# A four-layer graph network on one Trainium2 core: where the sums of a quantile search stand in TensorE's order, how many rows a constant has, and which engine makes the weights and second limits

## The chip, the core and the metric

The kernel runs on one core of a Trainium2 chip. The core has TensorE (PE in the profile; its weight loads are PEld), VectorE (DVE), ScalarE (ACT), GpSimd (POOL) and SyncE (SP, which here only issues DMAs). Each engine works through its own queue in order, and the engines wait for each other through semaphores. The metric is device time in microseconds (us).

## The reference, cut to what matters

Sixteen graphs of 1024 nodes and 64 channels go through four layers, each followed by a residual sum and a layer norm. Layer 0 is a normalised graph convolution, layer 1 an attention with eight heads, layer 3 a plain graph convolution. The change is in layer 2, which aggregates each node's neighbours by quantiles:

```
s = sort(where(nd, x, inf), over neighbours)     # nd: kept neighbours of a node
nv = nd.sum()                                     # their number
for tau, w in ((.25, .25), (.5, .5), (.75, .25)):
    pos = tau * max(nv - 1, 0)
    lo, hi, frac = floor(pos), ceil(pos), pos - floor(pos)
    agg += w * (s[lo] + frac * (s[hi] - s[lo]))
```

This is wanted for every node and every channel. So a pair of order statistics (`lo` and `hi`) is picked for each node, channel and one of three quantiles, and the two values are summed with the weights `w*(1-frac)` and `w*frac`.

## The kernel before, in words

The graphs are handled in pairs, eight pairs in all. One pass per pair runs layer 0, the attention, a sort of every channel over its nodes, and then the quantile search of the pair (`quantiles`, from line 880). Layers 2's small network and layer 3 of a pair are run beside layer 0 of a later pair.

**What the search does.** A channel's 1024 sorted values are cut into 32 groups of 32. A node's neighbours are a bit set over the ranks. A product of the adjacency matrix with a table `E` gives, for each node and channel, a *word*: a count of the neighbours below a group together with the bits of the group (three 16-bit words `V`). Comparing the counts with a *limit* (how many neighbours lie below the wanted order statistic) and taking differences gives a one-hot mark of the group that holds it (`lt`, then `oh`). The marked word is picked (`m = V * oh`), the 32 groups are summed (`wps`), and a bit search on VectorE (`kth_bit`) finds the place inside the group (`r2`, `r64`). From the place and the marks, products build a distance to every value of the group, ScalarE keeps what is positive (`vals`), and the sum over the group of these, together with the group's least value (`base`), is the wanted value (`acc`). The result is `acc * cf`, where `cf` is the weight.

**Steps and units.** One step treats four channels of one graph and one quantile. Eight steps form a unit; a pass has 12 units, that is 96 steps (`steps`, line 1065). The words of a step are picked 14 steps (`U8N + PARTS`) before its values are looked up. So one round `i` of the main loop (line 1116) holds, for TensorE: the sums of words of step `i-1` (`summed`, 12 products into `wps`); for the looked-up step the sums of least values (`least_values`, 4 products of `base` into `acc`), the distances (`distances`: 8 products with `pen`, 4 with `kilo`, 16 with `bd`, into four PSUM banks); one half word (`half_word`: a constant by the product `ones, magic`, then eight products `ndT, E`, into one bank); the first half of the one-hot marks of step `i+1` (`one_hot`, two products `lt, dif`, a bank each); the sums of values (`sum_values`, 4 products of `vals` with `bonesf` in float32 into `acc`); the second half of the marks; and in some rounds (three in eight) a second half word. The first step of a unit starts `acc` anew with its `least_values`, and for it these stand behind the first half of the marks, not ahead of the distances.

For VectorE a round is: the unit's result `acc * cf` if one is due (line 1055), two picks `m`, one comparison `lt` for step `i+2`, some of the next `E` tables, and, in the first six rounds of a unit, parts of `kth_bit`. ScalarE empties the PSUM banks: four `vals`, two reads of each half word into `V` (lines 947 to 953), four `oh`.

**What sets the order.** Products of the main loop go through `product`, which chains them in the order of the program, and VectorE's operations of the search go through `InOrder` (all recorded on line 749) in the same way. ScalarE's operations, and the weights and limits, are not chained: the scheduler places them. The four banks of pool `ps1` are handed out in turn, so the fifth use of a bank in a row waits for the eviction of the first. `m` has two buffers, so the first pick of a round waits for the sums of words of the round before. `acc` has one buffer.

**Limits and weights.** `rank_limits` (line 699) makes these of the neighbour counts. `limits(q)` writes `lim[:,0]` on ScalarE (line 717) and from it the two limits `s = 1, 0` on VectorE (line 719). `weights(t)` makes two 64-row `kc` and two `nvc` on ScalarE, their difference `d` on VectorE (line 731, buffer of the pool `vals`), its absolute value (line 732) and the weight `cf` (line 734), both on VectorE. For the first graph of a pair this is done ahead of the loop, but for two of the weights (rounds 10 and 12); for the second (`gr.bb` is 1) in the rounds of `SECOND`: counts in 26 and 28, weights in 30, 38 and 47, limits in 40, 45 and 46.

Of the kernel before, what the change touches and what calls it, by code (L numbers as in the profile page):

```python
# [15 lines left out]
BF = mybir.dt.bfloat16  # L16
# [4 lines left out]
AF = mybir.ActivationFunctionType  # L21
# [4 lines left out]
P = 128  # L26
# [7 lines left out]
EW = 2  # L34
# [87 lines left out]
def gnn_kernel(ctx: ExitStack, tc: tile.TileContext, a: dict, out: bass.AP):  # L122
# [52 lines left out]
    tones4 = load("tones4", [P, 4], F16, a["c_tones4"])  # L175
    kilo = const.tile([P, 1], F16, name="kilo")
    nc.vector.memset(kilo, 1024.0)
    magic = const.tile([32, EW, P], BF, name="magic")
    for w in range(EW):
        nc.vector.memset(magic[:, w], MAGIC[w] / 32)  # L180
    ones5 = const.tile([32, 512], BF, name="ones5")
    nc.vector.memset(ones5, 1.0)
    bn_a = const.tile([P, C], F32, name="bn_a")
    bn_b = const.tile([P, C], F32, name="bn_b")
# [514 lines left out]
    def rank_limits(gr, qe, qn, qm, behind):  # L699

        cnt = qe.tile([P, N], F16, name="cnt")
        gr.lim, gr.kc, gr.cf = {}, {}, {}

        def counts(hf):
            cols = slice(hf * 512, (hf + 1) * 512)
            ps = bank([P, 512])
            for j in range(NB):  # L710
                nc.tensor.matmul(ps, onesb, gr.ndT[:, j, cols], start=(j == 0), stop=(j == NB - 1))
            nc.scalar.copy(cnt[:, cols], ps)

        def limits(q):

            lim = gr.lim[q] = qe.tile([P, 2, N], U16, name="lim", bufs=LB)
            behind(nc.scalar.activation(lim[:, 0], cnt, AF.Copy, scale=0.25 * (q + 1), bias=-0.25 * (q + 1) - 0.375))
            for s in (1, 0):
                nc.vector.tensor_scalar(lim[:, s], lim[:, 0], 32.0, OFF + 32.0 * (s + 1), op0=ALU.mult, op1=ALU.add)

        def weights(t):
            nvc = qm.tile([P, 512], F16, name="nvc")
            kc = gr.kc[t] = qm.tile([P, 512], U16, name="kc", bufs=6)
            for hf in range(2):
                b = HALF[hf]
                x = cnt[b, hf * 512:(hf + 1) * 512]
                behind(nc.scalar.activation(kc[b], x, AF.Identity, scale=qrow[b, t, 0:1], bias=qrow[b, t, 1:2]))
                nc.scalar.activation(nvc[b], x, AF.Identity, bias=qrow[b, t, 4:5])

            d = qn.tile([P, 512], F32, name="vals", bufs=5)  # L730
            nc.vector.scalar_tensor_tensor(d, nvc, qrow[:, t, 0:1], kc, op0=ALU.mult, op1=ALU.subtract)
            nc.vector.scalar_tensor_tensor(d, d, -1.0, d, op0=ALU.mult, op1=ALU.max)
            cf = gr.cf[t] = qn.tile([P, 512], BF, name="cf", bufs=5)
            nc.vector.tensor_scalar(cf, d, qrow[:, t, 2:3], qrow[:, t, 3:4], op0=ALU.mult, op1=ALU.add)

        return counts, limits, weights

# [142 lines left out]
    def quantiles(ip, rk, u_w, b_w, qm, graphs):  # L880
# [12 lines left out]
        with ExitStack() as es:  # L893
# [93 lines left out]
            def summed(u, s):  # L987

                sum_words(u, s)
                if s == U8N - 1:  # L990
                    u.r2 = qn.tile([P, 512], F16, name="r2", bufs=2)
                    u.r64 = qn.tile([P, 512], F16, name="r64", bufs=2)
                    search = kth_bit(v, kb, u.wps, u.pairs[0][0].kc[u.n % 3], u.r2, u.r64)
                    next(search)
                    return search
# [51 lines left out]
            def result():  # L1047
                u = results.pop(0)
                gr = u.pairs[-1][0]
                res = qn.tile([P, 512], F32, name="vals", bufs=5)  # L1050
                if u is units[-1]:
                    nc.scalar.copy(res, u.acc)
                    nc.gpsimd.tensor_tensor(res, res, gr.cf[u.n % 3], ALU.mult)
                else:
                    searched[:] = [v.tensor_tensor(res, u.acc, gr.cf[u.n % 3], ALU.mult)]
                nc.gpsimd.dma_start(agg_d[gr.bb][:, u.n, :], res)
# [26 lines left out]
            def more_elements(n):  # L1083
                for _ in range(n):
                    if todo and made + 1 <= used // 2 + EB:
                        yield from elements()
# [25 lines left out]
            pen = qn.tile([P, U8N, 3, P], F16, name="pen")  # L1112
            nc.sync.dma_start(pen, a["c_pen"])
            lookups = [(gr, gb) for gr in graphs for gb in range(G // GB)]
            search = iter(())
            for i, (u, s) in enumerate(steps):
                if i == 3 * NQ:
                    load_matrix(graphs[1])
                if i == SECOND[0]:
                    counts, limits, weights = rank_limits(graphs[1], qe, qn, qm, behind)  # L1120
                if i in SECOND:
                    part, n = ((counts, 0), (counts, 1), (weights, 0), (weights, 1),
                               (limits, 0), (limits, 1), (limits, 2), (weights, 2))[SECOND.index(i)]
                    part(n)
                gb, at = divmod(i - U8N - 2 * NQ, GB * NQ)
                if at == 0 and gb >= 1 and lookups:
                    load_values(*lookups.pop(0))
                if i in (2, 4, 6):
                    load_values(*lookups.pop(0))
                if i in (10, 12):  # L1130
                    weights(i // 2 - 4)
                look = steps[i - U8N - PARTS] if i >= U8N + PARTS else None
                more = MORE[s] - (s == 3 and u.n % 3 == 2)
                if i:
                    search = summed(*steps[i - 1]) or search

                def large():
                    if results:
                        result()
                        yield  # L1140
                    pick(u, s, 0)
                    yield
                    pick(u, s, 1)
                    yield
                    if i + 2 < len(steps):
                        compare(*steps[i + 2])
                        yield
                    yield from more_elements(AT_ONCE[s] if i >= U8N else 2)

                runs = islice(search, RUNS[s] if s < PARTS else 0)  # L1150
                for _ in zip_longest(*((runs, large()) if s == PARTS - 1 else (large(), runs))):
                    pass
                if look and look[1]:
                    least_values(*look)
                if look:
                    distances(*look)
                more_words((more + 1) // 2)
                if i + 1 < len(steps):
                    one_hot(*steps[i + 1], 0)
                if look and not look[1]:  # L1160
                    least_values(*look)
                if look:
                    sum_values(*look)
                if i + 1 < len(steps):
                    one_hot(*steps[i + 1], 1)
                more_words(more // 2)
            search = summed(*steps[-1])
            before = None
            evicted.clear()
            for i, look in enumerate(steps[-U8N - PARTS:]):  # L1170
# [302 lines left out]
```

## Time and profile before

| | |
|---|---|
| three runs | 11837.91 us median (11832.29 to 11863.36) |
| profiled execution, its own time | 11843.83 us |
| its span, first to last instruction | 11842.1 us |
| busy in the span: PE, DVE, ACT | 10550.8, 10276.8, 7468.6 us |
| one search, first pick to last (first pair of graphs) | 1187.8 to 1972 us, about 784 us |
| mean granted TensorE clock | 0.958 |

In that first search (1187 to 1985 us) PE is busy 708.0 us of 798, DVE 756.0, ACT 526.8. A line of a waits view reads: who waited, for whom, microseconds in total, times, longest. A line of the timeline reads: start and duration in us, engine, line, operation, output<-inputs with shapes, count, and in brackets the idle time ahead of it and what ended it. A group's line has count, busy us, mean ns of one, and then the idle us ahead of its members with what ended them. Most instructions of the search have line 933 (PE) or 749 (DVE), those of the two helpers, so tiles tell them apart. The end of a matmul is modelled: starts are what can be relied on, and some matmul records are missing.

### The profile page before, as it was taken

To read this page: it belongs to the slowest core of one execution; us is meant where nothing else is said; L and a number is where in the kernel's file an instruction comes from. 1 tells how busy PE (TensorE), PEld (TensorE's weight loads), DVE (VectorE), ACT (ScalarE), POOL (GpSimd) and SP (SyncE) were. 2 spreads that over 40 slices of the span, in tenths; PEclk is the share of its full clock that TensorE was granted. 3 is DMA by queue.
4 is the path that set the end of the run, shared out by engine and by line. 5 is a ranking of instruction groups with operands and counts; after the bars stand their busy time and mean duration, and the time that the engine had idled before them with its cause. 6 is when DMAs were issued, how large, how long until landed. Compare 5 with 4: busy or idle time off the path is not lost.

```text
span 11842.1 us, 207662 instructions
## 1 busy us (share of the span) xinstructions
PE 10550.8 (89%) x81864; PEld 4573.6 (39%) x82560; DVE 10276.8 (87%) x18374; ACT 7468.6 (63%) x13812; POOL 712.4 (6%) x1212
## 2 busy tenths in 40 slices
PE   7989898998989989898898998989889998983897
PEld 4645232552335423354233542335322453221232
DVE  3588998889988899788997889988999889998996
ACT  5766666666666666566665666656666566661664
POOL 0010000000000000000000000010000100001000
PEclk8989999999999999999999999999999999996999
DMA  2021002210032000310004100041000410002001
GB/s 87 25 100 42 6 6 95 80 29 4 5 110 69 24 4 6 130 52 21 5 6 138 46 18 6 6 143 43 16 5 16 139 43 10 8 24 89 4 5 50
DMA packets 310001, 508.98 MB, mean 43 GB/s; under 512 B 120480, under 2 KB 220192, under 8 KB 306976
## 3 DMA queue, kind: packets, MB, share of 16 engines
q1 hardware_dynamic: 225296, 309.02, 8.3%
q0 software_dynamic: 50688, 99.75, 2.6%
q10 hardware_dynamic: 33040, 86.88, 2.2%
q8 instruction: 649, 10.63, 0.4%
q14 instruction: 328, 2.69, 0.1%
HBM read 379.03 MB, written 116.46 MB: 42 GB/s over the span
## 4 chain that ended last, share of the span: by engine, by line
PE 56%; DVE 27%; ACT 8%; issue 5%; DMA 3%; ACTq 0%; SPq 0%; DVEq 0%; POOL 0%
PE bank L933 19%; DVE m L749 8%; PE banks L549 7%; PE bank L571 7%; PE bank L585 7%; PE acc L933 5%; PE wps L933 3%; DVE S L749 3%; DVE lt L749 3%; ACT vals L1027 2%; DVE U L749 2%; DVE wb L749 2%; PE bank L414 1%; DVE key L1285 1%; PE bank L528 1%
## 5 line engine op out<-in xcount | busy, mean ns | idle before, releaser
L749 DVE TENSOR_TENSOR m<-V,oh 128x3072 bf16<-128x3072 bf16 x1536 | 2671.1, 1750 | 252.0 <-PE wps L933 219.1
L1027 ACT ACTIVATE vals<-bank 128x512 f32<-128x512 f32 x2848 | 1470.5, 602 | 1016.3 <-PE bank L933 1003.1
L933 PE MATMUL bank<-ndT,E 128*128 128x512 fp8e4 x7936 | 1942.2, 389 | 0.0
L556 DVE CUSTOM_DVE_ANT_0 s<-banks,adj 128x1024 f32<-128x1024 f32 x1024 | 1214.0, 1220 | 521.6 <-PE banks L549 516.4
L967 ACT CAST oh<-bank 128x512 f16<-128x512 f32 x3072 | 1591.0, 617 | 20.2 <-PE bank L933 18.6
L575 ACT COPY pT<-bank 128x512 f32<-128x512 f32 x1536 | 802.4, 593 | 812.2 <-PE bank L571 812.1
L564 ACT ACTIVATE s<-s,mx 128x1024 f32<-128x1024 f32 x1024 | 1176.4, 1160 | 98.6 <-DVE mx L556 95.9
L933 PEld LDWEIGHTS <-E 128*128 128x128 bf16 x7936 | 707.8, 99 | 1228.2 <-issue 551.2
L549 PE MATMUL banks<-kT,qT 64*128 64x512 f32 x4096 | 1113.0, 628 | 74.1 <-DVE mx L556 48.5
L571 PEld LDWEIGHTS bank<-ident,s 128*128 128x128 f32 x8192 | 900.6, 143 | 417.8 <-issue 289.7
L571 PE MATMUL bank<-ident,s 128*128 128x128 f32 x8192 | 1034.8, 280 | 8.4 <-ACT s L564 8.1
L933 PE MATMUL bank<-lt,dif 128*128 128x512 bf16 x2424 | 787.4, 383 | 262.9 <-issue 81.4
L585 PE MATMUL bank<-pT,v 128*64 128x256 f32 x8192 | 1003.8, 388 | 0.0
L749 DVE TENSOR_TENSOR lt<-V,lim 128x2048 bf16<-128x2048 uint16 x768 | 934.5, 1217 | 0.0
L933 PE MATMUL wps<-m,tonesb 128*32 128x512 bf16 x9216 | 660.8, 390 | 210.5 <-DVE m L749 208.2
L933 PE MATMUL bank<-oh,bd 64*64 64x512 f16 x11616 | 804.5, 388 | 0.0
L933 PE MATMUL acc<-vals,bonesf 128*32 128x512 f32 x5696 | 801.7, 611 | 2.2 <-ACT vals L1027 2.2
L585 PEld LDWEIGHTS bank<-pT,v 128*64 128x64 f32 x8192 | 548.1, 137 | 312.3 <-issue 47.9
L947 ACT ACTIVATE V<-bank 128x512 uint16<-128x512 f32 x512 | 305.4, 596 | 540.8 <-PE bank L933 476.8
L951 ACT ACTIVATE V<-bank 128x512 uint16<-128x512 f32 x512 | 305.5, 597 | 534.6 <-PE bank L933 533.9
L549 PEld LDWEIGHTS banks<-kT,qT 64*128 64x128 f32 x4096 | 400.1, 190 | 548.7 <-issue 341.2
L933 PE MATMUL bank<-r,pen 32*128 32x512 f16 x5808 | 587.4, 387 | 21.1 <-ACT vals L1027 13.1
(259 smaller groups left out, 14574.6 us busy)
## 6 DMA issues: line engine op xcount, KB each, us to landing
at<-in_adjT SPq DMA_DIRECT2D x256, 512.0 KB, 5.8
masks_d<-mask POOLq DMA_DIRECT2D x440, 128.0 KB, 2.0
mask<-masks_d SPq DMA_DIRECT2D x440, 128.0 KB, 2.1
adj<-in_adj SPq DMA_DIRECT2D x96, 512.0 KB, 6.0
ad<-in_adj ACTq DMA_DIRECT2D x64, 512.0 KB, 7.0
agg_d<-vals POOLq DMA_DIRECT2D x96, 256.0 KB, 2.3
agg<-agg_d ACTq DMA_DIRECT2D x16, 1536.0 KB, 7.6
nd_d<-nd SPq DMA_DIRECT2D x128, 128.0 KB, 2.1
```

The source lines that it names most:

```text
L549: then(nc.tensor.matmul(ss[h][:, hf * 512:(hf + 1) * 512], gr.qk[hp, 0][HALF[h], k * P:(k + 1) * P], gr.qk[hp, 1][HALF[h], hf * 512:(hf + ...
L556: last = nc.vector.tensor_tensor_reduce(s, ss[h], gr.adj[k], -1.0, 3.0e38, ALU.add, ALU.min, mx)
L564: then_act(nc.scalar.activation(s, s, AF.Exp, bias=mx, scale=-1.0, accum_out=sm))
L571: then(nc.tensor.transpose(ps[:, m, :], exps[h][0][:, (4 * mh + m) * P:(4 * mh + m + 1) * P], ident))
L575: then_act(nc.scalar.copy(dst, ps))
L585: then(nc.tensor.matmul(po[HALF[h]], gr.v[:, 4 * mh + m, (2 * hp + h) * C:(2 * hp + h + 1) * C], pT[h][mh][:, m, :], start=(mh == 0 and m ...
L749: i = getattr(nc.vector, name)(*args, **kw)
L933: then(nc.tensor.matmul(*args, **kw))
L947: nc.scalar.activation(gr.V[g][:, 0, cols], ps, AF.Copy, scale=2.0 ** -6, bias=OFF - MAGIC[0] / 64 - 63 / 128)
L951: nc.scalar.activation(gr.V[g][:, 2, cols], ps, AF.Copy, scale=2.0 ** -8, bias=OFF - MAGIC[1] / 256 - 255 / 512)
L967: nc.scalar.copy(u.oh[s][:, kk, cols], ps)
L1027: last = nc.scalar.activation(vals[t], ys[t], AF.Relu)
```

## The change

Four edits, the order of the first two being TensorE's own:

- The constant of a word, `magic`, gets 128 rows instead of 32 (each row a 128th of the constant instead of a 32nd), as does the vector of ones that it is multiplied with.
- The sums of values of a looked-up step stand one round later, right behind that round's sums of words; and the sums of least values (unless the step is its unit's first) right behind those, ahead of the round's vector work in the program. The unit's result on VectorE follows: it stands behind the two picks and the comparison, not ahead of them. After the loop one `sum_values` is still due and is issued behind the last sums of words.
- The two second limits of the second graph are made on ScalarE.
- The absolute value and the weight `cf` are made on ScalarE, for both graphs.

```diff
-    magic = const.tile([32, EW, P], BF, name="magic")
+    magic = const.tile([P, EW, P], BF, name="magic")
     for w in range(EW):
-        nc.vector.memset(magic[:, w], MAGIC[w] / 32)
-    ones5 = const.tile([32, 512], BF, name="ones5")
+        nc.vector.memset(magic[:, w], MAGIC[w] / P)
+    ones5 = const.tile([P, 512], BF, name="ones5")
...
             for s in (1, 0):
-                nc.vector.tensor_scalar(lim[:, s], lim[:, 0], 32.0, OFF + 32.0 * (s + 1), op0=ALU.mult, op1=ALU.add)
+                if gr.bb:
+                    nc.scalar.activation(lim[:, s], lim[:, 0], AF.Copy, scale=32.0, bias=OFF + 32.0 * (s + 1))
+                else:
+                    nc.vector.tensor_scalar(lim[:, s], lim[:, 0], 32.0, OFF + 32.0 * (s + 1),
+                                            op0=ALU.mult, op1=ALU.add)
...
             nc.vector.scalar_tensor_tensor(d, nvc, qrow[:, t, 0:1], kc, op0=ALU.mult, op1=ALU.subtract)
-            nc.vector.scalar_tensor_tensor(d, d, -1.0, d, op0=ALU.mult, op1=ALU.max)
+            nc.scalar.activation(d, d, AF.Abs)
             cf = gr.cf[t] = qn.tile([P, 512], BF, name="cf", bufs=5)
-            nc.vector.tensor_scalar(cf, d, qrow[:, t, 2:3], qrow[:, t, 3:4], op0=ALU.mult, op1=ALU.add)
+            nc.scalar.activation(cf, d, AF.Identity, scale=qrow[:, t, 2:3], bias=qrow[:, t, 3:4])
...
-            search = iter(())
+            search, before = iter(()), None
...
                 if i:
                     search = summed(*steps[i - 1]) or search
+                if before:
+                    sum_values(*before)
+                before = look
+                if look and look[1]:
+                    least_values(*look)
 
                 def large():
-                    if results:
-                        result()
-                        yield
                     pick(u, s, 0)
                     yield
                     pick(u, s, 1)
...
                         compare(*steps[i + 2])
                         yield
+                    if results:
+                        result()
+                        yield
                     yield from more_elements(AT_ONCE[s] if i >= U8N else 2)
...
-                if look and look[1]:
-                    least_values(*look)
                 if look:
                     distances(*look)
...
                 if look and not look[1]:
                     least_values(*look)
-                if look:
-                    sum_values(*look)
                 if i + 1 < len(steps):
                     one_hot(*steps[i + 1], 1)
                 more_words(more // 2)
             search = summed(*steps[-1])
+            sum_values(*before)
             before = None
```

## The prediction

> **What bounds the kernel.** The page first: PE and DVE are both busy nearly all the time, and the costliest group is DVE's pick.
>
> ```profile
> span 11842.1 us, 207662 instructions
> PE 10550.8 (89%) x81864; PEld 4573.6 (39%) x82560; DVE 10276.8 (87%) x18374; ACT 7468.6 (63%) x13812; POOL 712.4 (6%) x1212
> L749 DVE TENSOR_TENSOR m<-V,oh 128x3072 bf16<-128x3072 bf16 x1536 | 2671.1, 1750 | 252.0 <-PE wps L933 219.1
> ```
>
> The search is eight passes of about 784 us. Next the waits:
>
> ```profile
> DVE m L749 <- PE wps L933: 219.1, 144, 4.7
> PE wps L933 <- DVE m L749: 208.2, 169, 6.0
> PE bank L933 <- ACT V L949: 78.7, 59, 5.9
> PE bank L933 <- ACT V L953: 75.3, 72, 4.8
> ```
>
> PE and DVE wait for each other about equally: neither bounds alone. DVE's idle time ahead of picks is 31 us a pass. Pick by pick in the timeline of the first pass, the cycle is: DVE runs without idle from a unit's first pick through its round 5; PE waits for it around round 2, then runs without waiting for DVE to the unit's end, where DVE's next first pick waits 0.2 to 1.4 us. Then a round on PE:
>
> ```profile
> 1647.55 0.59 PE L933 MATMUL bank<-lt,dif 128*128 128x512 bf16 x2
> 1648.07 1.07 PE L933 MATMUL acc<-vals,bonesf 128*32 128x512 f32 x8
> 1649.30 0.38 PE L933 MATMUL bank<-lt,dif 128*128 128x512 bf16 x1 [0.16 <-issue]
> 1649.61 0.83 PE L933 MATMUL wps<-m,tonesb 128*32 128x512 bf16 x12
> 1650.27 0.39 PE L933 MATMUL acc<-oh,base 128*32 128x512 f16 x4
> 1650.59 0.83 PE L933 MATMUL bank<-r,pen 32*128 32x512 f16 x8
> 1651.57 1.06 PE L933 MATMUL bank<-oh,bd 64*64 64x512 f16 x16
> 1652.95 0.37 PE L933 MATMUL bank<-ones,magic 32*128 32x512 bf16 x1 [0.33 <-ACT vals L1027]
> ```
>
> (The third `dif`, at 1649.07, is a missing record.) The next round's first `dif` starts at 1654.99: 7.44 us. A round with two half words takes 9.60 (`bd` 1659.01 to 1668.62). PE's unit: 5 x 7.44 + 3 x 9.60 = 66.0; five regular units last 64.8 to 66.5. Both engines are critical, so what lengthens PE's round or links the two later costs time.
>
> **The change, part by part.**
>
> *Array shape.* Where the shape of PE's products changes (128*128 to 128*32, say) the next starts 0.31 after the last (1649.30 to 1649.61) and not the 0.22 of equal shapes (`E` to `E`). Moving the value sums beside the word sums, of the same shape, removes two changes from a round, and 128 rows for `magic` one more (`magic` to `E`); that from `bd` to `magic` is hidden already, `magic` waiting there for ScalarE (0.33). A second half word saves two more.
>
> *What takes the gain.* The value sums also gave ScalarE time: the fourth `dif` takes the bank of the half word, which needs both evictions into `V`. Without sums between, this wait is seen in the rounds before any look-up:
>
> ```profile
> 1213.07 0.81 PE L933 MATMUL bank<-lt,dif 128*128 128x512 bf16 x3
> 1214.41 0.38 PE L933 MATMUL bank<-lt,dif 128*128 128x512 bf16 x1 [0.53 <-ACT V L949]
> ```
>
> First to fourth `dif` is 1.34, not 0.65. The new round, start to start: four `dif` 1.34; to the word sums 0.31; these and on to the value sums 0.66; their two float32 passes 0.43 and, to `base`, 0.41; to `pen` 0.32; to `bd` 0.76 (as at 1675.82; 0.98 above, where the fourth bank still waited for an `oh` eviction, which is done by then); to `magic` 1.38; to `E` 0.22; to `dif` 1.73. Sum 7.56, against 7.44. With a second half word: `dif` to its `magic` 0.48 (seen at 1208.12, a wait for an `oh`), then 0.22 + 1.52 + 0.31: 9.78 against 9.60. So the round gets 0.12 to 0.18 longer, not 0.28 shorter.
>
> [...]
>
> *The result, later.* In a unit's round 6, `base` starts `acc` anew and waits for the result. Before, DVE made it ahead of its picks; now behind them:
>
> ```profile
> 1704.09 0.68 DVE L749 TENSOR_TENSOR vals<-acc,cf 128x512 f32<-128x512 f32 x1
> 1704.69 3.41 DVE L749 TENSOR_TENSOR m<-V,oh 128x3072 bf16<-128x3072 bf16 x2
> 1708.02 1.21 DVE L749 TENSOR_TENSOR lt<-V,lim 128x2048 bf16<-128x2048 uint16 x1
> 1717.04 1.76 DVE L749 TENSOR_TENSOR m<-V,oh 128x3072 bf16<-128x3072 bf16 x1 [0.94 <-PE wps L933]
> ```
>
> The unit from the pick at 1650.55: DVE runs 53.54 to 1704.09; picks and comparison take 4.55 (1704.69 to 1709.23), the result 0.60: 58.69. `base` can start at about 58.75; PE by its own rounds would be there at 57.65, so it waits 1.1. Then two `dif` and the word sums, 0.84; a round, 7.56; and 0.94 to the pick (1716.10 to 1717.04): 68.1 instead of 66.5. The same for the other regular units: +1.2, +1.2, +2.3, +2.4. Together +8.7 a pass. Behind `base` stand both last `dif` and all later PE work; the marks of round 7 come later too, but DVE's pick waits for the word sums anyway. The result's store on POOL is 4 us later; 0.55 to issue and 2.3 to land end before its buffer is used again in round 7, by about 1 us. No other DMA moves. One bound more: DVE's bit search starts with ScalarE's copy of `wps`, now closer behind the `oh` evictions, 0 to 0.3 a unit; I take 0.
>
> *Weights on ScalarE.* DVE is rid of 0.68 and 0.54 per weight. What ScalarE takes is not in the trace: 0.60 each by `vals` (128x512 out of PSUM), 0.81 by `kc` (scale and bias by row, but 64 rows); I take 0.60 for the absolute value and 0.7 for `cf`, and the difference, 0.2 on six weights a pass, matters only where ScalarE is late. In rounds 29 and 37 ScalarE stood still for DVE, because the next weight's `nvc` waited for `d`:
>
> ```profile
> 1494.42 0.72 ACT L728 ACTIVATE nvc<-cnt,qrow 64x512 f16<-64x512 f16 x1 [6.29 <-DVE vals L731]
> 1496.16 0.59 PE L933 MATMUL bank<-lt,dif 128*128 128x512 bf16 x1 [5.81 <-ACT V L949]
> ```
>
> PE stood with it, its clock fell (E's eight took 3.59, not 1.90), DVE lost 4.7 and 4.3 ahead of the first picks of rounds 30 and 38, and 3 more in the two rounds after each. In the built program's order the absolute value takes that place in round 29, and `d` stands two `E` operations (1.2) later: the stall goes on and is 1.2 longer, less 0.2 for shape changes; with the result's wait the unit takes +1.7. In round 37 the order is other: the `V` and `oh` evictions stand ahead of the absolute value. Then the word sums follow at about 1492.6 and not at 1500.7, and the wait moves to `pen` (for the second half word's evictions, 1498.1); the first pick of round 39 comes at 1504.7 and not at 1509.8, -5.
>
> *Limits on ScalarE.* DVE saves 0.34 each (0.42 less overlap), twice per limit; ScalarE does two more of 1.06 in a row. Behind round 39's they hold up `vals` by 1.2 to 2 (before, `vals` at 1511.28 just cleared the first at 1509.84); those of 45 and 46 by 1.3 and 1.7, partly in PE's slack of round 44 (0.49 waited). So unit 32 to 39 is -5 + 1.2 + about 0.8 for the colder clock = -3, and unit 40 to 47, with its result, +1.
>
> *Nothing.* Weights ahead of the loop: DVE then waits 2.03 for `oh`, so its saving hides there; two more ScalarE operations cost 0 to 1.2, I take 0. Rounds 10 and 12: DVE saves 2.4, but round 15 already waits for PE (0.2 to 1.3). Wider memsets run once at the start. In the last two units DVE already waits for PE (rounds 85 to 87 and 94): +0.8 and +0.5 by the longer rounds.
>
> **Sum.** Per pass 8.7 + 1.7 - 3 + 1 + 1.3 = +9.7, times 8 = +78. The profiled execution took 11843.8, 6 above the median of 11837.9; on that median I predict 11915.
>
> **Rivals.**
> - *PE's gain is real* (faster): if `V` is evicted in time because ScalarE starts sooner, rounds shorten by 0.28 to 0.46. Then DVE's idle of regular units (0.9 each, five), the 5 of round 37, and 1 at the end go, less the limits' 2: -8 a pass, 11774. For it: 0.31 against 0.22, seen hundreds of times. Against: the wait in every early round. It decides if four `dif` take under 1.0.
> - *Lost in slack* (same): DVE's work stays the unit's length, and the result's wait falls in PE's slack (PE waits 208 for picks, 2.2 a unit). Then only the two stalls count, +1.7 - 3 + 1: -2 us in all, 11836. Against: PE has no slack from round 3 on.
> - *ScalarE's queue bites more* (much slower): round 37's stall stays (+1.2 and not -5), limits cost 2 each, the copy of `wps` 0.3 a unit: 9.7 + 6.2 + 2 + 2.5 = 20 a pass, 12000. For it: 5 and 6 us stalls from one waiting operation; against: the order in round 37.
>
> **How the numbers follow.** Forecast 0.50, ScalarE's queue 0.17, slack 0.20, gain 0.13. A measurement of this kernel tells 0.3% (36 us) from no change. Faster is the gain's 0.13; same is slack and little of the forecast: 0.20; slower 0.67. The range takes in ScalarE's case and slack with half of the gain: 11800 to 12010; the forecast's own is 11870 to 11960.
>
> **What would show it.** `dif` waiting for `V` up from 154 us to some 450; first to fourth `dif` 1.34; `base` of round 6 waiting about 1 us for the result; PE's round 7.56; the first pick of round 38 without its 4.3, that of round 30 with more than 4.7; DVE's wait for `wps` up. If four `dif` take 0.65, or `base` waits for nothing, I am wrong in sign.

## The result, and the profile after

| | before | after |
|---|---|---|
| median of four runs | 11843.2 us (11832.3 to 11863.4) | 11964.9 us (11956.4 to 11968.6) |
| ratio, with its 95% interval | | 1.0098 (1.0082 to 1.0114) |
| span of the profiled execution | 11842.1 us | 11954.7 us |
| one search, first pick to last, mean of eight passes | 782.9 us | 798.3 us |

The changed kernel is 121.7 us slower. The eight searches are 15.4 longer each, 123 together; outside them the spans differ by 10 the other way.

The page of the changed kernel: its totals, and the group of the picks with its idle time and what ended it.

```profile
span 11954.7 us, 208208 instructions
PE 10361.0 (87%) x82505; PEld 4693.6 (39%) x82560; DVE 10228.3 (86%) x18230; ACT 7572.2 (63%) x13956; POOL 711.3 (6%) x1212
L753 DVE TENSOR_TENSOR m<-V,oh 128x3072 bf16<-128x3072 bf16 x1536 | 2673.4, 1752 | 391.8 <-PE wps L937 317.0 <-ACT oh L971 55.0 <-issue 17.0
```

PE and DVE are both less busy in a longer span: neither has more work, both wait more. The picks' own 2673.4 us are unchanged; the idle time ahead of them is 391.8 and was 252.0. The waits of the changed kernel name who is late:

```profile
DVE m L753 <- PE wps L937: 317.0, 176, 6.9
PE bank L937 <- ACT V L957: 251.7, 343, 6.2
PE bank L937 <- ACT V L953: 174.9, 317, 1.3
ACT vals L736 <- DVE vals L735: 92.0, 39, 5.9
PE acc L937 <- DVE vals L753: 68.2, 42, 2.8
```

Products wait 426.6 us for the evictions into `V`, 406.5 of it in `dif` and the rest in `pen` (154.0 before, all in `dif`), and `base` 68.2 for the result, a wait that the kernel before had not. ScalarE's absolute value (L736) stands 92.0 waiting for `d`, where ScalarE's `nvc` stood 99.1 before. The timeline of TensorE, in rounds 53 and 54 of the first pass (in the brackets: idle time, and what ended it):

```profile
1639.66 0.81 PE L937 MATMUL bank<-lt,dif 128*128 128x512 bf16 x3
1640.99 0.38 PE L937 MATMUL bank<-lt,dif 128*128 128x512 bf16 x1 [0.52 <-ACT V L957]
...
1649.21 0.59 PE L937 MATMUL bank<-lt,dif 128*128 128x512 bf16 x2
1650.68 0.40 PE L937 MATMUL acc<-oh,base 128*32 128x512 f16 x4 [0.87 <-DVE vals L753]
```

The first line to the second is the 1.33 of a round whose value sums no longer stand between its marks. The last is `base` of round 54, which starts `acc` anew and waits until DVE, behind two picks and a comparison, has made the result:

```profile
1645.46 3.42 DVE L753 TENSOR_TENSOR m<-V,oh 128x3072 bf16<-128x3072 bf16 x2
1648.80 1.22 DVE L753 TENSOR_TENSOR lt<-V,lim 128x2048 bf16<-128x2048 uint16 x1
1649.94 0.68 DVE L753 TENSOR_TENSOR vals<-acc,cf 128x512 f32<-128x512 f32 x1
...
1659.98 1.76 DVE L753 TENSOR_TENSOR m<-V,oh 128x3072 bf16<-128x3072 bf16 x1 [1.88 <-PE wps L937]
```

In two of a pass's units without weights or limits (16 to 23 and 64 to 71), which have one half word less, PE comes to `base` earlier and waits longer (round 70 of the first pass):

```profile
1786.64 0.40 PE L937 MATMUL acc<-oh,base 128*32 128x512 f16 x4 [2.81 <-DVE vals L753]
1786.97 0.60 PE L937 MATMUL bank<-lt,dif 128*128 128x512 bf16 x2
1787.51 1.38 PE L937 MATMUL wps<-m,tonesb 128*32 128x512 bf16 x12
1788.66 1.93 PE L937 MATMUL acc<-vals,bonesf 128*32 128x512 f32 x8
```

The word sums then take 1.38 and not 0.83, the value sums 1.93 and not 1.03. The windows of that stretch (length, each engine's busy time with its count, then PE's granted clock, DMA share and GB/s) show why: the granted clock was 0.58 behind the wait (0.50 for 3.41 us of it, from 1787.65), and 1.00 before and after:

```profile
1779.00:1787.00 8.00, 4.87 (x48) 1.88 (x45) 7.93 (x10) 3.15 (x6) 0.12 (x1) 1.00 0.01 2
1787.00:1791.00 4.00, 4.00 (x34) 0.97 (x34) 2.65 (x4) 2.05 (x4) 0.44 (x1) 0.58 0.17 66
1791.00:1799.00 8.00, 7.21 (x81) 2.63 (x77) 5.27 (x5) 5.86 (x11) 0.00 (x0) 1.00 0.00 0
```

### The profile page after: what moved, and what is told of

Same layout as the page of the kernel before. It is cut to its first block, busy times and chain, and to the rows that moved or that the text cites. A ratio compares the mean times of both kernels' runs of the same rounds, so it can differ in the third digit from the quotient of the medians.

```text
span 11954.7 us, 208208 instructions
## 1 busy us (share of the span) xinstructions
PE 10361.0 (87%) x82505; PEld 4693.6 (39%) x82560; DVE 10228.3 (86%) x18230; ACT 7572.2 (63%) x13956; POOL 711.3 (6%) x1212
## 4 chain that ended last, share of the span: by engine, by line
PE 47%; DVE 29%; ACT 11%; issue 9%; DMA 3%; POOL 0%; ACTq 0%; SPq 0%; DVEq 0%; POOLq 0%
PE bank L937 12%; DVE m L753 8%; PE banks L549 8%; PE bank L571 7%; PE bank L585 7%; PE acc L937 3%; DVE lt L753 3%; DVE S L753 3%; PE wps L937 2%; DVE U L753 2%; DVE wb L753 2%; ACT vals L1031 2%; ACT oh L971 2%; PE bank L528 1%; DMA at<-in_adjT 1%
## 5 line engine op out<-in xcount | busy, mean ns | idle before, releaser
L753 DVE TENSOR_TENSOR m<-V,oh 128x3072 bf16<-128x3072 bf16 x1536 | 2673.4, 1752 | 391.8 <-PE wps L937 317.0
L937 PE MATMUL bank<-ndT,E 128*128 128x512 fp8e4 x7936 | 1914.3, 385 | 0.4
L937 PE MATMUL bank<-lt,dif 128*128 128x512 bf16 x3072 | 939.6, 381 | 435.2 <-ACT V L957 231.6
L937 PEld LDWEIGHTS <-E 128*128 128x128 bf16 x7936 | 781.4, 98 | 1175.2 <-issue 374.8
L937 PE MATMUL acc<-vals,bonesf 128*32 128x512 f32 x5696 | 757.1, 606 | 0.0
L937 PE MATMUL bank<-ones,magic 128*128 128x512 bf16 x985 | 378.0, 384 | 262.2 <-ACT vals L1031 235.5
```

The costliest lines, as they stand in the source:

```text
L753: i = getattr(nc.vector, name)(*args, **kw)
L937: then(nc.tensor.matmul(*args, **kw))
```

## The experiments

Two tables hold what was measured. In the first, "six units" are those of a pass without weights, limits or start and end (16 to 23, 48 to 87); each number is the time from a unit's first pick to the next unit's, in us, a mean over the eight passes of the profiled execution. The time is the median of the runs, the ratio that to the kernel before on the same chip.

| kernel | time, us | ratio (95% interval) | six units | 24-31 | 32-39 | 40-47 | pass |
|---|---|---|---|---|---|---|---|
| before | 11841 to 11848 | 1 | 394.6 | 75.7 | 74.4 | 67.5 | 782.9 |
| whole change | 11964.9 | 1.0098 (1.0082, 1.0114) | 408.8 | 77.3 | 72.8 | 69.3 | 798.3 |
| e1_constant | 11787.9 | 0.9959 (0.9946, 0.9972) | 390.8 | 74.4 | 73.7 | 68.2 | 777.7 |
| e2_scalar | 11936.1 | 1.0078 (1.0065, 1.0091) | 394.7 | 76.1 | 77.0 | 75.1 | 793.9 |
| e3_order | 11990.8 | 1.0121 (1.0106, 1.0136) | 409.8 | 78.5 | 71.3 | 70.4 | 801.7 |
| e4_result | 11903.8 | 1.0051 (1.0037, 1.0065) | 399.0 | 77.0 | 73.6 | 73.4 | 791.7 |
| e5_next_weight | 11700.5 | 0.9871 (0.9856, 0.9886) | 390.6 | 69.2 | 67.9 | 68.2 | 766.3 |
| e6_weights_only | 11903.2 | 1.0044 (1.0029, 1.0059) | 394.6 | 76.2 | 75.0 | 73.3 | 790.4 |
| e7_limits_only | 11873.7 | 1.0025 (1.0015, 1.0035) | 394.7 | 75.7 | 76.2 | 69.5 | 786.5 |
| e8_marks_first | 12026.5 | 1.0146 (1.0131, 1.0161) | 411.5 | 76.4 | 78.6 | 69.9 | 807.2 |
| e9_rounds_moved | 11707.5 | 0.9890 (0.9874, 0.9906) | 392.3 | 67.4 | 68.4 | 67.4 | 765.2 |
| e10_both_waits | 12007.3 | 1.0140 (1.0124, 1.0157) | 403.9 | 76.9 | 79.0 | 73.7 | 803.5 |
| e11_bank_sooner | 11819.5 | 0.9981 (0.9972, 0.9990) | 395.2 | 71.2 | 73.1 | 72.8 | 780.9 |
| e12_control | 11792.5 | 0.9957 (0.9940, 0.9974) | 391.5 | 75.2 | 73.9 | 67.7 | 778.0 |

The second is PE's round, from the start of its word sums to that of the next ones, in a unit's round 0 (one half word) and round 1 (two), means over four units (48 to 63, 72 to 87) of each pass:

| | before | e1 | e3 | whole change | e4 | e8 | e10 | e11 | e12 |
|---|---|---|---|---|---|---|---|---|---|
| one half word | 7.44 | 7.32 | 7.65 | 7.56 | 7.54 | 7.42 | 7.41 | 7.30 | 7.40 |
| two half words | 9.59 | 9.29 | 9.97 | 9.77 | 9.77 | 9.36 | 9.36 | 9.51 | 9.55 |

### The constant alone

```diff
-    magic = const.tile([32, EW, P], BF, name="magic")
+    magic = const.tile([P, EW, P], BF, name="magic")
...
-        nc.vector.memset(magic[:, w], MAGIC[w] / 32)
-    ones5 = const.tile([32, 512], BF, name="ones5")
+        nc.vector.memset(magic[:, w], MAGIC[w] / P)
+    ones5 = const.tile([P, 512], BF, name="ones5")
```

> The kernel before with one edit, the constant of a word and its vector of ones on 128 rows. My theory (the value sums between the two halves of the marks cover the evictions into V, so a saved shape change is real time there): 0.09 us less in each of a unit's rounds 3 to 7, 0.19 less for each second half word among them, together 0.6 to 0.8 a unit, which is less than the 0.9 that VectorE idles ahead of a regular unit's first pick; ten units in eight passes give 45 to 65 us less, about 11790 where the kernel before takes 11843. First to fourth dif stays at 0.65, the waits of dif for V stay near 154 us. Rival (shape changes lie in slack, or what PE saves it waits for ScalarE): within 15 us of before, with the waits of bank for V or for vals grown by what the shape changes saved.

Measured: 56 us less, as the theory has it. The round is 0.12 shorter with one half word and 0.30 with two. The waits for `V` are almost as before (164.8 us), and PE now waits more for DVE and DVE less for PE than before (208.2 and 219.1):

```profile
PE wps L933 <- DVE m L749: 273.5, 208, 6.2
DVE m L749 <- PE wps L933: 181.3, 107, 4.5
PE bank L933 <- ACT V L949: 86.6, 70, 6.4
PE bank L933 <- ACT V L953: 78.2, 72, 5.0
```

One word of the expectation was wrong: with the value sums between, first to fourth `dif` is 1.75, here and before; 0.65 is what is left of it without the sums. Shape changes are real time where the round's waits are covered.

### The order alone, and the order without the result's wait

`e3_order` is the kernel before with:

```diff
...
+                if before:
+                    sum_values(*before)
+                before = look
+                if look and look[1]:
+                    least_values(*look)
 
                 def large():
-                    if results:
-                        result()
-                        yield
                     pick(u, s, 0)
...
+                    if results:
+                        result()
+                        yield
                     yield from more_elements(AT_ONCE[s] if i >= U8N else 2)
...
-                if look and look[1]:
-                    least_values(*look)
...
-                if look:
-                    sum_values(*look)
...
             search = summed(*steps[-1])
+            sum_values(*before)
```

`e4_result` is the changed kernel with:

```diff
                 def large():
+                    if results:
+                        result()
+                        yield
                     pick(u, s, 0)
...
-                    if results:
-                        result()
-                        yield
                     yield from more_elements(AT_ONCE[s] if i >= U8N else 2)
...
                 if look and not look[1]:
                     least_values(*look)
+                if look and look[1] == U8N - 1:
+                    sum_values(*look)
+                    before = None
                 if i + 1 < len(steps):
                     one_hot(*steps[i + 1], 1)
```

> The kernel before with the moved sums, least values and result alone; constant on 32 rows, weights and limits on VectorE. My theory (this edit carries the whole loss; the fourth dif waits for both evictions into V, and base of a unit's round 6 waits for the result): 150 to 190 us more than before, more than the whole change costs, since the other two edits give some back; waits of dif for V near 430 us, base waiting for the result near 68 us in all. Rival (the loss comes from ScalarE's new work, or from the edits together): less than 80 us more.

> The changed kernel, but the value sums of a unit's last looked-up step stay in their own round between the halves of the marks, and the result stands ahead of the next round's picks, as before; the other seven steps keep the new place. My theory (two causes, of which this takes away the wait for the result): base then waits for nothing, the 1.9 us of idle time ahead of a unit's first pick becomes about 1, and each unit gets some 0.8 shorter: 55 to 75 us less than the changed kernel, still 40 to 70 more than before. Rival A (the wait for the result lies beside the wait for V or for the picks): no more than 15 us less than the changed kernel. Rival B (the wait for the result is the whole loss): no slower than before.

Measured: the order alone costs 147 us, close to the range, more than the whole change. Its waits:

```profile
PE bank L933 <- ACT V L953: 240.2, 343, 6.1
PE bank L933 <- ACT V L949: 166.5, 305, 1.2
PE acc L933 <- DVE vals L749: 56.5, 32, 2.3
```

Unit 32 to 39 is 3.1 shorter than before all the same. ScalarE's timeline at round 37 of the first pass, where the next weight's `nvc` now stands behind the evictions:

```profile
1498.96 2.06 ACT L967 CAST oh<-bank 128x512 f16<-128x512 f32 x4
1503.50 1.45 ACT L728 ACTIVATE nvc<-cnt,qrow 64x512 f16<-64x512 f16 x2 [2.47 <-DVE vals L731]
```

Without the result's wait the changed kernel is 61 us quicker, and still 60 slower than before. In the six units that wait is worth 9.8 us of the 14.2 by which the change lengthens them; 4.4 remain, and PE's round is as long as in the whole change. (Unit 40 to 47 got 4.1 longer in this kernel: the absolute value came to stand elsewhere in ScalarE's queue, see below.)

### Weights and limits on ScalarE, together and each alone

On the kernel before, `e7_limits_only` has the first part of this diff, `e6_weights_only` the second and `e2_scalar` both:

```diff
             for s in (1, 0):
-                nc.vector.tensor_scalar(lim[:, s], lim[:, 0], 32.0, OFF + 32.0 * (s + 1), op0=ALU.mult, op1=ALU.add)
+                if gr.bb:
+                    nc.scalar.activation(lim[:, s], lim[:, 0], AF.Copy, scale=32.0, bias=OFF + 32.0 * (s + 1))
+                else:
...
...
-            nc.vector.scalar_tensor_tensor(d, d, -1.0, d, op0=ALU.mult, op1=ALU.max)
+            nc.scalar.activation(d, d, AF.Abs)
...
-            nc.vector.tensor_scalar(cf, d, qrow[:, t, 2:3], qrow[:, t, 3:4], op0=ALU.mult, op1=ALU.add)
+            nc.scalar.activation(cf, d, AF.Identity, scale=qrow[:, t, 2:3], bias=qrow[:, t, 3:4])
```

> The kernel before with the weights and the second limits on ScalarE, TensorE's order and the constant as they were. My theory: the stall of 4.3 us ahead of the first pick of round 38 goes (5 us less in that unit), the one of 4.7 ahead of round 30's stays and grows by about 1.2, and the limits give 1 to 2 back; 2 to 5 us a pass, 15 to 40 us less in all. Rival (ScalarE's queue, with operations that wait for VectorE, holds up evictions more than VectorE gains): 10 to 40 us more, with both stalls still there.

> The kernel before with the absolute value and the weight alone on ScalarE (limits on VectorE, TensorE's order as before). My theory, from e2_scalar's units: the absolute value stands ahead of urgent evictions and waits for d, 0.4 us more in unit 24 to 31, 0.5 to 1.5 more in 32 to 39 and about 2.5 in 40 to 47, less 0.9 in 8 to 15: 15 to 35 us more than before. Rival (the weights carry e2_scalar's loss): 70 us or more.

> The kernel before with the second graph's two second limits alone on ScalarE. My theory, from e2_scalar's units: 2 us more in unit 32 to 39 (limits behind round 39's marks hold up vals) and about 5 in 40 to 47, since a stop of 2 us is followed by a fall of TensorE's clock: 45 to 70 us more than before. Rival (only the 1 to 2 us that the limits hold up, as the prediction priced them, and nothing after it): 20 us or less.

Measured: together 92 us slower, where the theory had 15 to 40 faster and the rival 10 to 40 slower. The weights alone cost 55, between the theory's 15 to 35 and the rival's 70 (by its interval 34 to 70); the limits alone 26, under the theory's 45 and above the rival's 20, which its interval of 18 to 41 doesn't shut out. In `e7_limits_only` the granted clock stayed at 1.00 from 1552 to 1580 us of the first pass, where limits are made twice, with TensorE idle for 2.67 of the 6 us from 1560: the fall that its theory put behind a stop of 2 us did not come there. The loss is in the three units that hold this work. ScalarE's timeline of `e6_weights_only`, round 46 of the third pass:

```profile
4466.44 2.06 ACT L1027 ACTIVATE vals<-bank 128x512 f32<-128x512 f32 x4
4473.83 0.63 ACT L732 ACTIVATE vals<-vals 128x512 f32<-128x512 f32 x1 [5.32 <-DVE vals L731]
4474.50 0.81 ACT L734 ACTIVATE cf<-vals,qrow 128x512 bf16<-128x512 f32 x1
4475.22 0.57 ACT L947 ACTIVATE V<-bank 128x512 uint16<-128x512 f32 x1
```

The absolute value stands ahead of the evictions into `V` and waits 5.32 for `d`, which DVE makes behind two picks and a comparison; DVE then loses nearly as much, 4.62:

```profile
4473.05 0.75 DVE L731 SCALAR_TENSOR_TENSOR vals<-nvc,qrow,kc 128x512 f32<-128x512 f16 x1
4478.43 3.43 DVE L749 TENSOR_TENSOR m<-V,oh 128x3072 bf16<-128x3072 bf16 x2 [4.62 <-PE wps L933]
```

In the whole change the same operation, in the same round, stands behind the evictions, and waits 0.78:

```profile
4485.00 2.06 ACT L971 CAST oh<-bank 128x512 f16<-128x512 f32 x4
4487.84 0.63 ACT L736 ACTIVATE vals<-vals 128x512 f32<-128x512 f32 x1 [0.78 <-DVE vals L735]
```

So the parts don't add up: -56, +92 and +147 make +183, the whole is +122, and unit 40 to 47 accounts for all of that and more: its excesses of 0.7, 7.5 and 2.9 sum to 11.1, and in the whole it has 1.8. That is 9.3 a pass, 75 in all. By these timelines it is where the scheduler puts one waiting operation that decides; no run changes that place alone.

### The stall that both kernels have

`e1_constant`'s kernel, and:

```diff
-                nc.scalar.activation(nvc[b], x, AF.Identity, bias=qrow[b, t, 4:5])
+                behind(nc.scalar.activation(nvc[b], x, AF.Identity, bias=qrow[b, t, 4:5]))
```

> The constant on 128 rows as in e1_constant, and one more edit: the two nvc of a weight, too, stand behind the round's picks, as its kc do, so that none of the next weight stands on ScalarE ahead of urgent evictions while it waits for d. My theory (the stalls ahead of the first picks of rounds 30 and 38, 4.7 and 4.3 us, are that one waiting operation): both shrink to 1 to 2 us, for kc and nvc then stand four in a row, 1.3 longer than the two kc; units 24 to 31 and 32 to 39 get 3 to 6 us shorter each; 11690 to 11740, that is 50 to 100 less than e1_constant. Rival (d itself comes late, and something else waits for it in the same place): within 15 us of e1_constant's 11788, the idle time ahead of both picks unchanged.

(`behind` ties an operation to the round's last pick.) Measured: 11700.5, in the theory's range, 1.3% faster than before and the lowest median here (its interval and that of `e9_rounds_moved`, below, overlap). ScalarE's timeline of the kernel before at round 29 of the first pass, with the next weight's `nvc` between `vals` and the evictions into `V`:

```profile
1412.40 2.07 ACT L1027 ACTIVATE vals<-bank 128x512 f32<-128x512 f32 x4
1419.78 0.72 ACT L728 ACTIVATE nvc<-cnt,qrow 64x512 f16<-64x512 f16 x1 [5.31 <-DVE vals L731]
1420.40 0.57 ACT L951 ACTIVATE V<-bank 128x512 uint16<-128x512 f32 x1
```

And the same place in this kernel:

```profile
1410.82 0.81 ACT L727 ACTIVATE kc<-cnt,qrow 64x512 uint16<-64x512 f16 x1
1411.54 0.71 ACT L728 ACTIVATE nvc<-cnt,qrow 64x512 f16<-64x512 f16 x1
1412.26 0.81 ACT L727 ACTIVATE kc<-cnt,qrow 64x512 uint16<-64x512 f16 x1
1412.97 0.70 ACT L728 ACTIVATE nvc<-cnt,qrow 64x512 f16<-64x512 f16 x1
1413.70 2.07 ACT L1027 ACTIVATE vals<-bank 128x512 f32<-128x512 f32 x4
1416.49 0.60 ACT L951 ACTIVATE V<-bank 128x512 uint16<-128x512 f32 x1 [0.72 <-PE bank L933]
```

No line waits for DVE, and the first picks of rounds 30 and 38 have no idle time ahead of them. Units 24 to 31 and 32 to 39 are 5.2 and 5.8 shorter than in `e1_constant`.

`e9_rounds_moved` tried to get what is left:

```diff
-SECOND = (26, 28, 30, 38, 40, 45, 46, 47)
+SECOND = (24, 26, 32, 34, 40, 45, 46, 48)
```

> e5_next_weight with the second graph's parts in other rounds: counts in 24 and 26 (were 26, 28), weights in 32, 34 and 48 (were 30, 38, 47), limits as they were in 40, 45, 46. These rounds are the first three of a unit, where TensorE waits for VectorE's picks and ScalarE's queue has slack. My theory (what is left of the stalls, 4.2, 2.9 and 3.2 us in the three units against a regular one of about 65, is work of ScalarE and TensorE in rounds without slack): 5 to 9 us less a pass, 40 to 70 less than e5_next_weight, 11630 to 11660. Rival (what is left is VectorE's own work, which only changes places): within 15 us of e5_next_weight.

Measured: 11707.5, within 15 us: the rival is right on the time. Units 24 to 31 and 40 to 47 gain 1.8 and 0.8, while the six units and 32 to 39 lose 1.7 and 0.5.

### Is the wait for V real time?

`e8_marks_first` is the changed kernel, `e10_both_waits` is `e4_result`, each with:

```diff
-                more_words((more + 1) // 2)
                 if i + 1 < len(steps):
                     one_hot(*steps[i + 1], 0)
+                more_words((more + 1) // 2)
```

> The changed kernel with the first half of the marks ahead of the half word instead of behind it, so that the half word's eight products lie between the two halves and no dif takes a bank whose evictions into V are still under way. My theory (the fourth dif's wait for V is real time): dif's waits for V fall from 427 us to under 100; in their place the first two dif wait for the evictions of vals, 0.3 to 0.7 a round; in sum 0 to 60 us less than the changed kernel, and not back to before. Rival A (the wait for V lies beside other waits): no change of time though the waits are gone. Rival B (the new wait is the longer one): 20 us or more above the changed kernel.

> The changed kernel with both edits, e4_result's (a unit's last value sums and the result at their old places) and e8_marks_first's (first half of the marks ahead of the half word). In e8_marks_first TensorE's rounds were shorter (7.42 and 9.36 us against 7.56 and 9.77) and the unit was not, which leaves open if the wait for V is real time. My theory (there the result set the unit's length; with that gone the shorter rounds count): regular units fall from e4_result's 65.5 to 67.4 to 64.8 to 66.2, 30 to 80 us less than e4_result, 11825 to 11875. Rival (the marks ahead of the half word hold up VectorE's picks by themselves): no less than 11890.

Measured: both are slower than what they came from, by 62 and 104 us: rival B in the first and the rival in the second. The waits for `V` went (87 us are left in the first) and the rounds of the table got shorter, by 0.14 and 0.41, but the units did not. The unit's round with `base` (62 of the first pass of `e8_marks_first`) shows what came instead:

```profile
1730.49 0.40 PE L937 MATMUL acc<-oh,base 128*32 128x512 f16 x4 [1.44 <-DVE vals L753]
1730.82 0.39 PE L937 MATMUL bank<-lt,dif 128*128 128x512 bf16 x1
1731.57 0.38 PE L937 MATMUL bank<-lt,dif 128*128 128x512 bf16 x1 [0.36 <-ACT oh L971]
```

PE arrives earlier, waits longer for the same result, and then for an `oh`; the new order brings stalls of its own. In the searches of the profiled executions the granted clock was at 0.50 for 495 us in `e8_marks_first`, where the changed kernel has 280, and for 433 in `e10_both_waits`, where `e4_result` has 263, so part of the loss may be the clock's. The pair doesn't answer the question. The last pair does it without another order on TensorE; `e11_bank_sooner` is `e4_result` and `e12_control` the kernel before, each with:

```diff
                 if w == 0:
...
+                    low = gr.V[g][:, 0, cols].bitcast(U8).rearrange("p (n b) -> p n b", b=2)[:, :, 0]
                     nc.scalar.activation(both[:, :, 1], low, AF.Copy, scale=0.25, bias=OFF / 256)
                 else:
...
+                    low = gr.V[g][:, 2, cols].bitcast(U8).rearrange("p (n b) -> p n b", b=2)[:, :, 0]
                     nc.scalar.copy(both[:, :, 0], low)
```

> e4_result (the changed kernel without the wait for the result), but ScalarE's second read for V takes the first one's output in V instead of the bank, so that the bank comes free one operation sooner while ScalarE does as many operations. This changes what is computed: the low bytes of the words are another value. My theory (the fourth dif's wait for V is real time, and is what is left of the loss): first to fourth dif falls from 1.34 to about 0.9, the waits of dif for V from 420 us to under 200, regular units from 65.5 to 67.4 to 64.8 to 66.3; 40 to 90 us less than e4_result's 11904. Rival (the wait lies in slack, as the longer units of e8_marks_first and e10_both_waits could be read): no more than 20 us less, beyond what e12_control gains.

> The kernel before with the same edit to the second read alone, as a control (the low bytes of the words are another value here too). In its rounds the value sums already cover the evictions into V; what waits for them is 154 us, mostly in the rounds ahead of any look-up and in those with weights. My theory: 0 to 25 us less than before. Rival (the edit helps in another way, by quicker reads or another order on ScalarE): 40 us less or more.

Measured: first to fourth `dif` falls from 1.34 to 0.85, the waits for `V` from 419.8 to 85.9, and the round by 0.24 and 0.26, where the control's falls by 0.04: within a round the wait is real time. But the control gained 51 us, twice what I gave it at most, so its rival is right, and of the 84 that `e11_bank_sooner` gained over `e4_result` only some 33 are the difference. By the intervals of the ratios that is uncertain by almost as much (17, 11 and 20 us, some 28 together). The control's gain is seen in `pen` behind a second half word, which waits for the same evictions (its eight mostly take 0.61 in place of 0.83 to 1.06).

The first table shows where the difference lies. `e11_bank_sooner` gains 10.8 a pass on `e4_result` and the control 4.9 on the kernel before, 5.9 apart. Of this, 0.7 are in the six units (3.8 and 3.1) and 5.3 in unit 24 to 31 (5.8 and 0.5). There the edit changed ScalarE's order: in round 29 the absolute value, which waits 5.89 for `d` in `e4_result`, stands behind evictions and waits 1.99, and the idle time ahead of the first pick of round 30 (6.64 in the first pass of `e4_result`) is gone:

```profile
1420.38 1.55 ACT L973 CAST oh<-bank 128x512 f16<-128x512 f32 x3
1423.92 0.63 ACT L736 ACTIVATE vals<-vals 128x512 f32<-128x512 f32 x1 [1.99 <-DVE vals L735]
```

In `e11_bank_sooner` the picks also wait for ScalarE in another place:

```profile
PE wps L937 <- DVE m L753: 393.4, 236, 6.6
DVE m L753 <- ACT oh L973: 200.6, 116, 4.7
DVE m L753 <- PE wps L937: 39.0, 25, 4.1
```

How much of the loss is the wait for `V` alone stays open. This pair differs by some 33 us, between nothing and 60 within its uncertainty, and by the table that is for the most part a stall that went with ScalarE's new order, not the shorter rounds.

## Why the prediction was right, and where it was off

The sign and the main mechanism held; the rise was 122 and not 78. Of the 5.7 us a pass that the sum lacked, 4.4 are in the term of the result.

- *Shape changes.* Priced at 0.09 each; the constant alone, one change less a round and two more per second half word, gave 0.12 and 0.30, some 0.1 a change. That one edit of the four, by itself, gave 11788, where nothing else stood in the way.
- *What takes the gain.* First to fourth `dif` 1.34, the round 7.56 and 9.77 (forecast 7.56 and 9.78), the waits for `V` 427, 407 of them `dif`'s (forecast 450). `e3_order` shows that the order alone makes the round 7.65 and 9.97, and that the constant takes back 0.09 and 0.20. Shown to be real in the round; its share of the total stays open, as said.
- *The result, later: the term that was mis-sized.* Forecast +8.7 a pass in five units, measured +13.1. The wait of `base` is 0.8 to 1.0 in three of them (forecast 1.1), and 2.8 in the two with fewer half words, units 16 to 23 and 64 to 71. There the step failed: I let PE run on at its full clock. Behind the 2.8 it fell to 0.50 in 12 of 16 cases, and these units got +3.8 and +4.4, not the forecast's largest terms of +2.3 and +2.4. The passes give the price: unit 16 to 23 took 67.5 where the clock held (+2.7), 69.0 with one fall of 3.41 us and 70.4 with one of 6.83. By that, an estimate, the clock has some 2.6 of the 4.4 us a pass. Much of the rest may be the copy of `wps`, which I had bounded at 0 to 0.3 a unit and taken as 0: it is 0.27 in most units (DVE's waits for it went from 8 to 87), 1.4 in five if each wait passes on whole. Here `e4_result` is the test: 9.8 of 14.2 in the six units go with the result's place, and in them its clock stays at 1.00.
- *Weights on ScalarE.* Round 29's stall stayed and grew (idle ahead of round 30's first pick 4.71 before, 6.29 after), and the unit took +1.6, as forecast +1.7. Round 37's went, and the unit took -1.6 in the mean of the passes (-3.0 in the first; forecast -3). The built order that the prediction read for round 37 was right; the edit that it was put down to was not. I had credited the edit on ScalarE, but the weights alone leave that stall (75.0 for 74.4), and `e3_order` loses it with the weights on VectorE (71.3). In its trace, shown above, the evictions into `V` and `oh` of round 37 stand ahead of the waiting `nvc`, whose wait is 2.47 there and was 6.29: with TensorE's new order the scheduler put ScalarE's operations in another. The prices themselves were near: the absolute value takes 0.63 (I took 0.60), `cf` 0.82 (0.7), both medians of 48 in the changed kernel.
- *Limits on ScalarE.* Unit 40 to 47 forecast +1, measured +1.8. Alone they cost 26 us. The weight of round 47 stands in this unit too and had no term: alone it made the unit 5.8 longer (`e6_weights_only`), in the whole change its absolute value stands behind the evictions. That it could be left out was luck.
- *Nothing.* Unit 8 to 15 gained 0.9, where I had taken the two weights of rounds 10 and 12 as hidden; the last two units took +1.1 and +0.7 (forecast +0.8 and +0.5).
- *Rivals.* "PE's gain is real" fell where the whole change is meant, by the four `dif`; it is right of the constant alone. "Lost in slack" fell: the rounds' length and the result's wait reached the time. "ScalarE's queue bites more" is right in kind of `e2_scalar` (+92): round 37's stall stays there, as the rival says, but most of the loss is in unit 40 to 47, which it hadn't named. In the whole change ScalarE's operations stand in another order in rounds 37 and 46, and it did not come.

## What to carry to other kernels

A saved shape change on TensorE was worth its 0.1 us here (0.12 a round in `e1_constant`) only while nothing waited behind it: before products are brought together, ask what the ones that are moved away were covering, here two reads of a bank by ScalarE. An operation that waits for a slow engine, in the in-order queue of an engine that frees banks, cost about its wait here where it stood ahead of evictions (5.3 us of wait made a unit 5.8 longer in `e6_weights_only`; without the waits of 5.4 and 6.7 that `e1_constant` has, two units are 5.2 and 5.8 shorter in `e5_next_weight`); look for such lines with several us of idle time in the kernel as it is, since tying two of them to a place where they don't wait (`behind`) was worth 87 us on top of the constant's 56. And where a scheduler places an engine's operations, an edit on one engine moves stalls on another: compare the built order, and don't add up the prices of parts.

## What the runs showed of the hardware that was not expected

A wait of TensorE of 2.81 us (2.53 in one case) was enough for its granted clock to fall from 1.00 to 0.50 for 3.41 us or twice that: of the 16 waits of `base` in rounds 22 and 70 of the changed kernel, 12 were followed or met by such a fall (8 of 8 in round 70, 4 of 8 in round 22), none of the waits of 1.04 and less. In `e3_order` waits of 2.17 to 2.27 us were enough in 17 of 24 cases (rounds 22, 46 and 70). The forecast's term for this wait had no such fall in it; and with the same wait it came not every time.

What tells these 40 waits apart is where they lie. In both traces the changes of the granted clock stand whole multiples of 3.41 us apart. The 29 waits that put 2.02 us or more of idle time into one such stretch met a fall, and the 11 that put 1.96 or less into any did not. So the same wait of 2.81 us made unit 16 to 23 last 67.5 us in four passes, and 69.0 to 70.4 in the other four.
